# A selective scan: the products with B on GpSimd, those with C on VectorE, decay and states in PSUM

## The chip, the cores and the metric

The kernel runs on one core of a Trainium2 chip. A core has a matrix engine (TensorE, "PE" in the profile, its weight loads "PEld"), VectorE ("DVE"), ScalarE ("ACT"), GpSimd ("POOL") and SyncE ("SP", which issues the DMAs here). Each runs its own list of instructions in order and waits on semaphores for the others. [...] The metric is the device time of one execution, in microseconds. The kernel before takes 18,649.57 us, the median of three runs (18,648.17 to 18,655.98).

## The reference

The input is 2 images of 96 channels and 128 x 128 points. Layer 0 normalizes over the channels and adds a mixing step: four Mamba scans (along rows, along columns, and both in reverse), each with 192 inner channels and 16 states a channel, whose outputs are projected and summed. A feed-forward net of 96, 384 and 96 with quantized numbers follows; layer 1 is a 3 x 3 convolution and another such net. Only the scan matters here:

```python
dt = softplus(dt_raw @ dt_w.T + dt_b)          # per channel and point
dA = exp(dt[:, :, None] * A)                   # A = -exp(A_log), 16 per channel
h  = dA * h + dt[:, :, None] * B[:, None, :] * u[:, :, None]
y  = einsum('bds,bs->bd', h, C)                # sum over the 16 states
y  = y + Dp * xc                               # the skip; xc is u
y  = y * silu(z)
return y @ outp_w.T
```

B and C (16 values a point each) and `dt_raw` are projections of `xc`, which is the Silu of a causal convolution of four taps over the projected input.

## The kernel before

Each image goes through three stages: `normalize`, `mamba` (the scans) and `ffn_and_conv`. The sum over the four directions is kept in `acc` in SBUF.

`mamba` runs the four directions as two pairs: rows with columns, forward, then both in reverse. A pair has 384 channels, three groups (`NG`) of 128 partitions; group 1 holds 64 channels of each direction. A step is 512 points of one pair (`T`), so there are 64 steps an image and 128 in all. A step has 24 units: a unit is one group and two of the 16 states, worked on as tiles of 128 x 2 x 512.

A unit before the change (`inputs_of` and `scans`, lines 277 to 301):

- TensorE broadcasts the two B rows to all partitions by matmuls with 0/1 weights `sel` into the PSUM tile `bc` (L282). B is split in three bf16 parts, `parts`, for accuracy (L229 to L239).
- ScalarE makes the decay `da` = exp(dt x A) in SBUF, one instruction a state (L285).
- VectorE multiplies `bc` by `dtu` = dt x u in place (L290) and runs two scans over the 512 points (L293), which write the states `h` in SBUF.
- ScalarE copies the last point's state to `hst`, for the next step (L297).
- GpSimd multiplies `h` by the C rows `cs` (L299). `cs` comes by DMA: the C rows are written to DRAM (L222) and read back, broadcast to 128 partitions (L274), three units ahead (`AHEAD`).
- TensorE adds the product to the group's sum `y` in PSUM by a matmul with the identity (L301).

After a group's eight units `finish` (L303) adds the skip on VectorE (L308), multiplies by the gate on GpSimd (L309) and, after groups 1 and 2, projects with TensorE and adds into `acc` with VectorE (L318, L320, L326).

The inputs of a step (`prologue`, L185) are made in the step before, piece by piece: after each unit one more piece of a generator is written. It loads two input tiles (L196), runs the convolution as 16 matmuls (L182), Silu (L206), the gates (L211), the projections to C rows (L218) and to B and dt (L228), and per group the softplus (L246 to L260), of which ScalarE makes Abs, Relu, Exp and Ln, VectorE a rounding step `q` (L255), and GpSimd three sums and `dtu` (L258 to L262). ScalarE loads another function table before the Silus and back after them (L206, L213).

What sets the order: every engine but ScalarE gets its instructions from a planner, which starts from the written order and may move an instruction that it holds to be ready ahead of one that waits; ScalarE keeps the written order in `mamba` (L329). Waits follow from which instructions touch which tiles. [...]

Of the kernel before, what the change touches and what calls it, by code (L numbers as in the profile page):

```python
# [1 line left out]

# [17 lines left out]
C = 96  # L20
# [11 lines left out]
AHEAD = 3  # L32
DTO = 96
# [3 lines left out]
def tile_metaformer(ctx: ExitStack, tc: tile.TileContext, a: dict, out: bass.AP):  # L37
# [21 lines left out]
    bdw = const("bdw", (128, 2, NG, DTO + 2 * RK))  # L59
    cw = const("cw", (128, 2, NG, 2 * S))  # L60
    dtw = const("dtw", (2 * RK, 2, NG * 128))
    dtb = const("dtb", (128, 2, NG))
    dskip = const("dskip", (128, 2, NG))
# [4 lines left out]

    amat = cpool.tile([128, 2, NG, S], F32, name="amat")
    sel = cpool.tile([96, S, 2, 128], BF16, name="sel")  # L70
# [3 lines left out]
    with tc.tile_pool(name="prep", bufs=1) as pp, tc.tile_pool(name="prep_ps", bufs=2, space=PSUM) as pps:  # L74
# [4 lines left out]
        onehot = pp.tile([96, 2, S], F32, name="onehot")  # L79
        nc.sync.dma_start(onehot, a["onehot"])  # L80
        for d in range(2):
            nc.vector.tensor_copy(sel[:, :, d, :], onehot[:, d, :, None].broadcast_to((96, S, 128)))
# [75 lines left out]
    def mamba(acc, xnr, xnc):  # L158

        with ExitStack() as st:  # L160
            pool = lambda n, bufs, **kw: st.enter_context(tc.tile_pool(name=n, bufs=bufs, **kw))
            io, one, two, gen = pool("io", 2), pool("one", 1), pool("two", 2), pool("gen", 6)
            ps_bc, ps_y, ps_m = (pool(n, k, space=PSUM) for n, k in (("ps_bc", 2), ("ps_y", 1), ("ps_m", 3)))
# [21 lines left out]
            def prologue(pi, i, d):  # L185

                rev = pi == 1
                lo = L - (i + 1) * T if rev else i * T
                src = []
                for n, dram in (("xa", xnr), ("xb", xnc)):  # L190
                    t = io.tile([C, T + 3], F32, name=n)
                    if i == 0:
                        nc.gpsimd.memset(t[:, T : T + 3] if rev else t[:, 0:3], 0.0)
                        nc.sync.dma_start(t[:, 0:T] if rev else t[:, 3 : T + 3], dram[:, lo : lo + T])
                    else:
                        nc.sync.dma_start(t, dram[:, lo : lo + T + 3] if rev else dram[:, lo - 3 : lo + T])  # L196
                    src.append(t[:, ::-1] if rev else t)
                yield
                d["xc"], d["sz"], d["dt"], d["dtu"] = [], [], [], []
                ps = []  # L200
                for g in range(NG):
                    ps.append(inproj(pi, g, lambda dd, k, lo, hi: inx[:, dd, k, lo:hi], src, (0, 1, 2, 3)))
                    yield
                for g in range(NG):
                    xc = gen.tile([128, T], F32, name="xc")
                    nc.scalar.activation(xc, ps[g], AF.Silu, bias=convb[:, pi, g : g + 1])  # L206
                    d["xc"].append(xc)
                for g in range(NG):
                    z = inproj(pi, g, lambda dd, k, lo, hi: inz[:, dd, lo:hi], src, (3,))
                    sz = gen.tile([128, T], F32, name="sz", bufs=5)  # L210
                    nc.scalar.activation(sz, z, AF.Silu)  # L211
                    d["sz"].append(sz)
                nc.scalar.preload_act_table_set("natural_log_exp_and_others")  # L213
                yield

                ps = misc()
                for g in range(NG):
                    nc.tensor.matmul(ps[0 : 2 * S, :], cw[:, pi, g, :], d["xc"][g], start=g == 0, stop=g == NG - 1)  # L218
                crow = one.tile([2 * S, T], F32, name="crow")
                nc.scalar.copy(crow, ps[0 : 2 * S, :])  # L220
                d["cd"] = rows_d.tile([2 * S, T], F32, name="cd")
                nc.sync.dma_start(d["cd"], crow)  # L222
                yield


                ps = misc()
                for g in range(NG):
                    nc.tensor.matmul(ps[0 : DTO + 2 * RK, :], bdw[:, pi, g, :], d["xc"][g], start=g == 0, stop=g == NG - 1)  # L228
                parts = two.tile([96, T], BF16, name="parts")  # L229
                nc.scalar.copy(parts, ps[0:96, :])  # L230
                rest = one.tile([96, T], F32, name="rest")
                nc.vector.tensor_tensor(rest, ps[0:96, :], parts, ALU.subtract)
                dtr = one.tile([2 * RK, T], F32, name="dtr")
                nc.scalar.copy(dtr, ps[DTO : DTO + 2 * RK, :])
                yield
                mid = one.tile([96, T], BF16, name="mid")
                nc.gpsimd.tensor_copy(mid, rest)
                nc.vector.tensor_copy(parts[32:64, :], mid[32:64, :])
                nc.gpsimd.tensor_tensor(parts[64:96, :], rest[64:96, :], mid[64:96, :], ALU.subtract)  # L239
                d["parts"] = parts  # L240
                yield


                for g in range(NG):
                    ps = misc()
                    nc.tensor.matmul(ps, dtw[:, pi, g * 128 : (g + 1) * 128], dtr, start=True, stop=True)  # L246
                    bias = dtb[:, pi, g : g + 1]
                    e = one.tile([128, T], F32, name="e")
                    nc.scalar.activation(e, ps, AF.Abs, bias=bias)
                    dt = gen.tile([128, T], F32, name="dt", bufs=4)  # L250
                    nc.scalar.activation(dt, ps, AF.Relu, bias=bias)  # L251
                    nc.scalar.activation(e, e, AF.Exp, scale=-1.0)
                    yield
                    q = one.tile([128, T], F32, name="q")
                    nc.vector.tensor_scalar(q, e, 1.0, 1.0, ALU.add, ALU.subtract)  # L255
                    ln = one.tile([128, T], F32, name="ln")
                    nc.scalar.activation(ln, e, AF.Ln, bias=1.0)
                    nc.gpsimd.tensor_tensor(q, e, q, ALU.subtract)  # L258
                    nc.gpsimd.tensor_tensor(ln, ln, q, ALU.add)  # L259
                    nc.gpsimd.tensor_tensor(dt, dt, ln, ALU.add)  # L260
                    dtu = gen.tile([128, T], F32, name="dtu", bufs=4)
                    nc.gpsimd.tensor_tensor(dtu, dt, d["xc"][g], ALU.mult)  # L262
                    d["dt"].append(dt)
                    d["dtu"].append(dtu)
                    yield

            def c_rows(d, g, s):

                cs = gen.tile([128, 2, T], F32, name="cs", bufs=4)
                for half in range(2) if g == 1 else (slice(None),):  # L270
                    rows = slice(half * 64, half * 64 + 64) if g == 1 else half
                    at = s + S * (half if g == 1 else g // 2)
                    n = 64 if g == 1 else 128
                    nc.sync.dma_start(cs[rows], d["cd"][None, at : at + 2, :].broadcast_to((n, 2, T)))  # L274
                return cs

            def inputs_of(pi, d, g, s):

                bp = ps_bc.tile([128, 2, T], F32, name="bc")
                for j in range(2):  # L280
                    w = sel[:, s + j, :, :].rearrange("k d m -> k (d m)")[:, 64 * g : 64 * g + 128]
                    nc.tensor.matmul(bp[:, j, :], w, d["parts"], start=True, stop=True)  # L282
                da = two.tile([128, 2, T], F32, name="da")
                for j in range(2):
                    nc.scalar.activation(da[:, j, :], d["dt"][g], AF.Exp, scale=amat[:, pi, g, s + j : s + j + 1])  # L285
                return bp, da

            def scans(i, d, g, s, y, cs, bp, da):

                nc.vector.tensor_tensor(bp, d["dtu"][g][:, None, :].broadcast_to((128, 2, T)), bp, ALU.mult)  # L290
                h = two.tile([128, 2, T], F32, name="h")
                for j in range(2):
                    nc.vector.tensor_tensor_scan(  # L293
                        h[:, j, :], da[:, j, :], bp[:, j, :],
# [3 lines left out]
                hc = two.tile([128, 2, T], F32, name="hc")  # L298
                nc.gpsimd.tensor_tensor(hc, h, cs, ALU.mult)  # L299
                for j in range(2):  # L300
                    nc.tensor.matmul(y, ident, hc[:, j, :], start=s + j == 0, stop=s + j == S - 1)  # L301

            def finish(pi, i, d, g, y):  # L303

                rev = pi == 1
                lo = L - (i + 1) * T if rev else i * T
                t = one.tile([128, T], F32, name=f"yg{g}")
                nc.vector.scalar_tensor_tensor(t, d["xc"][g], dskip[:, pi, g : g + 1], y, ALU.mult, ALU.add)  # L308
                nc.gpsimd.tensor_tensor(t, t, d["sz"][g], ALU.mult)  # L309
                d["yg"].append(t[:, ::-1] if rev else t)  # L310
                yg = d["yg"]
# [22 lines left out]
            for _ in prologue(*steps[0], state[0]):  # L334
                pass
            cs = {k: c_rows(state[0], *units[k]) for k in range(AHEAD)}
            got = inputs_of(steps[0][0], state[0], *units[0])
            for n, (pi, i) in enumerate(steps):
# [3 lines left out]
                for u, (g, s) in enumerate(units):  # L342
# [7 lines left out]
                    else:  # L350
                        for _ in ahead:
                            pass
# [157 lines left out]
```

## Time and profile before

| | us |
|---|---|
| median of three runs | 18,649.57 |
| the profiled execution | 18,639.52 |
| its span, first to last instruction | 18,637.7 |
| VectorE busy | 12,812.0 |
| TensorE busy (matmuls) | 14,287.1 |
| GpSimd busy | 10,041.0 |
| ScalarE busy | 6,766.3 |

The 40 slices of the page show where the stages are. Two long even stretches are the scans of the two images; the short ones between and at the end, in which GpSimd is nearly idle, are the feed-forward nets with the convolution:

```profile
DVE  4777777777777777753347777777777777777533
POOL 2666666666666666630026666666666666666300
DMA  2333333333333333310023333333333333333100
```

In a line of the groups, the part before the first bar says what instruction it is (line, engine, operation, tile written <- tiles read, shapes, count), then come busy us in total and mean ns of one, then the idle time of that engine just before such instructions and whom it waited for. Busy time counts a stretch once, also where two instructions of an engine overlap.

### The profile page before, as it was taken

Reading aid. Unit: us, or ns where it says so; the run is one execution under the profiler, and the core shown is the slowest. Engines: PE = TensorE matmul, PEld = TensorE weight load, DVE = VectorE, ACT = ScalarE, POOL = GpSimd, SP = SyncE. Lnnn points to the kernel's source line nnn. Section 1 sums busy time; section 2 is a strip of 40 time slices with the busy share of each in tenths; the row PEclk is TensorE's granted clock in tenths of the full one; section 3 lists DMA queues with packets and bytes.
Section 4 is the critical chain, followed back from the end, with each engine's and each line's share of the span. In section 5 each row is a group of like instructions: output and inputs, shape, how many; then the busy total and the mean of one; then the engine's idle time right before and its main releaser. Section 6 shows DMA issues by size and latency. Waiting matters only on the chain. (4 is left out here: it accounts for less than half of the span.)

```text
span 18637.7 us, 119806 instructions
## 1 busy us (share of the span) xinstructions
PE 14287.1 (77%) x33424; PEld 5080.7 (27%) x33424; DVE 12812.0 (69%) x12267; ACT 6766.3 (36%) x13205; POOL 10041.0 (54%) x5412
## 2 busy tenths in 40 slices
PE   6777777777777777777767777777787777777777
PEld 2222222222222222223322222222222222222233
DVE  4777777777777777753347777777777777777533
ACT  2433333343333433422223433333333334334222
POOL 2666666666666666630026666666666666666300
PEclk7888998899988888877778889988888888888777
DMA  2333333333333333310023333333333333333100
GB/s 87 109 105 108 108 107 108 105 108 108 107 106 106 106 106 106 107 55 6 6 85 106 108 106 108 108 107 106 106 107 107 104 107 106 108 106 106 54 6 6
DMA packets 511015, 1732.76 MB, mean 93 GB/s; under 512 B 75612, under 2 KB 76988, under 8 KB 505640
## 3 DMA queue, kind: packets, MB, share of 16 engines
q1 hardware_dynamic: 510344, 1725.11, 29.9%
q8 instruction: 263, 4.31, 0.1%
q14 instruction: 408, 3.34, 0.1%
HBM read 1678.68 MB, written 46.14 MB: 93 GB/s over the span
## 5 line engine op out<-in xcount | busy, mean ns | idle before, releaser
L299 POOL TENSOR_TENSOR hc<-h,cs 128x1024 f32<-128x1024 f32 x3072 | 7245.3, 2362 | 5219.9 <-DVE h L293 3434.5
L301 PE MATMUL y<-hc,ident 128*128 128x512 f32 x12288 | 7260.5, 722 | 2487.3 <-POOL hc L299 2456.2
L293 DVE TENSOR_TENSOR_SCAN h<-da,hst,bc 128x512 f32<-128x512 f32 x5952 | 7218.0, 1262 | 211.0 <-ACT da L285 72.9
L290 DVE TENSOR_TENSOR bc<-dtu,bc 128x1024 f32<-128x1024 f32 x3072 | 3685.8, 1219 | 2206.1 <-PE bc L282 2198.5
L301 PEld LDWEIGHTS y<-hc,ident 128*128 128x128 f32 x12288 | 2534.1, 224 | 6549.6 <-POOL hc L299 4297.4
L285 ACT ACTIVATE da<-dt,amat 128x512 f32<-128x512 f32 x6144 | 4080.7, 712 | 1.5
L297 ACT COPY hst<-h 128x2 f32<-128x2 f32 x3072 | 586.0, 191 | 7922.3 <-DVE h L293 7922.1
L282 PE MATMUL bc<-parts,sel 96*128 96x512 bf16 x6144 | 1970.8, 396 | 571.7 <-DVE h L293 568.4
L416 POOL TENSOR_TENSOR acc<-acc,y 96x512 f32<-96x512 f32 x128 | 147.0, 1148 | 2158.8 <-DVE y L415 2158.8
L282 PEld LDWEIGHTS <-sel 96*128 96x128 bf16 x6144 | 598.6, 102 | 2583.7 <-issue 2521.4
L182 PE MATMUL misc<-xa,inx 96*128 96x512 f32 (+1 forms) x2048 | 1054.8, 611 | 64.0 <-issue 32.2
L182 PE MATMUL misc<-xb,inx 96*64 96x512 f32 (+1 forms) x2048 | 1047.6, 610 | 0.3 <-ACT dt L251 0.3
L308 DVE SCALAR_TENSOR_TENSOR yg<-xc,dskip,y 128x512 f32<-128x512 f32 x384 | 285.3, 743 | 745.8 <-PE y L301 745.8
L309 POOL TENSOR_TENSOR yg<-yg,sz 128x512 f32<-128x512 f32 x384 | 485.5, 1264 | 543.9 <-DVE yg L308 486.8
L431 PE MATMUL pc<-pad,kw 96*96 96x512 f32 x1152 | 663.0, 699 | 48.2 <-DVE pad L129 48.2
L126 PE MATMUL pr<-sd,bcast_w 128*96 128x128 f32 x2048 | 450.1, 390 | 313.5 <-DVE sd L123 309.5
L114 ACT ACTIVATE sq<-xm 96x512 f32<-96x512 f32 x256 | 161.0, 629 | 1202.6 <-DVE xm L112 1161.1
L211 ACT ACTIVATE sz<-misc 128x512 f32<-128x512 f32 x384 | 229.3, 597 | 996.7 <-POOL yg L309 656.3
L260 POOL TENSOR_TENSOR dt<-dt,ln 128x512 f32<-128x512 f32 x384 | 490.9, 1278 | 20.2
L259 POOL TENSOR_TENSOR ln<-ln,q 128x512 f32<-128x512 f32 x384 | 485.5, 1264 | 30.1
L262 POOL TENSOR_TENSOR dtu<-dt,xc 128x512 f32<-128x512 f32 x384 | 486.6, 1267 | 27.8
L258 POOL TENSOR_TENSOR q<-e,q 128x512 f32<-128x512 f32 x384 | 484.7, 1262 | 9.6 <-DVE q L255 9.6
(88 smaller groups left out, 9731.6 us busy)
## 6 DMA issues: line engine op xcount, KB each, us to landing
cs<-cd SPq DMA_DIRECT2D x2048, 512.0 KB, 3.7
cs<-cd SPq DMA_DIRECT2D x2048, 256.0 KB, 3.9
xa<-xnr SPq DMA_DIRECT2D x124, 193.1 KB, 3.4
xb<-xnc SPq DMA_DIRECT2D x124, 193.1 KB, 4.0
acc<-in_x_dram SPq DMA_DIRECT2D x16, 768.0 KB, 16.2
xnr<-xn SPq DMA_DIRECT2D x16, 768.0 KB, 4.3
xnc<-st SPq DMA_DIRECT2D x16, 768.0 KB, 4.6
out_dram<-acc SPq DMA_DIRECT2D x64, 192.0 KB, 2.1
```

The source lines that it names most:

```text
L182: nc.tensor.matmul(ps[rows, :], w(PAIRS[pi][d], k, lo, hi), src[d][:, k : k + T], **se)
L259: nc.gpsimd.tensor_tensor(ln, ln, q, ALU.add)
L260: nc.gpsimd.tensor_tensor(dt, dt, ln, ALU.add)
L262: nc.gpsimd.tensor_tensor(dtu, dt, d["xc"][g], ALU.mult)
L282: nc.tensor.matmul(bp[:, j, :], w, d["parts"], start=True, stop=True)
L285: nc.scalar.activation(da[:, j, :], d["dt"][g], AF.Exp, scale=amat[:, pi, g, s + j : s + j + 1])
L290: nc.vector.tensor_tensor(bp, d["dtu"][g][:, None, :].broadcast_to((128, 2, T)), bp, ALU.mult)
L293: nc.vector.tensor_tensor_scan(h[:, j, :], da[:, j, :], bp[:, j, :], 0.0 if i == 0 else hst[:, g, s + j : s + j + 1], ALU.mult, ALU.add,)
L297: nc.scalar.copy(hst[:, g, s : s + 2], h[:, :, T - 1])
L299: nc.gpsimd.tensor_tensor(hc, h, cs, ALU.mult)
L301: nc.tensor.matmul(y, ident, hc[:, j, :], start=s + j == 0, stop=s + j == S - 1)
L431: nc.tensor.matmul(pc, kw[:, t, :], rows, start=t == 0, stop=t == 8)
```

## The change

- The B and C rows now both come by DMA. One projection (`bcw`) makes dt, B and C together; B and C rows alternate in DRAM (`bcd`), and a unit's load is four rows, B and C of two states, into one SBUF tile `bc` of 128 x 2 x 2 x 512. Five such tiles are in turn, and loads are issued three units ahead (`ROWS_AHEAD`). The broadcast by TensorE, `sel`, `parts`, `rest` and `mid` go.
- GpSimd multiplies B by `dtu`, in place in `bc`, two units ahead (`AHEAD`).
- `da` is a PSUM tile (three of two banks, six of the eight banks). The scans write the states over it, and VectorE multiplies them with C, in place in `bc`.
- Four units of 24 (`BY_POOL`) are treated otherwise: their scans write the states over B in SBUF, and GpSimd makes the product with C one unit later.
- The skip is a matmul of `xc` with a diagonal matrix `dmat`, which starts the sum `y`; the gate is then one product on VectorE (`gated`), after the first unit of the next group. Projection and adding into `acc` come two and three units after a group.
- The pieces of the prologue are tied to fixed units by a table (`at`). Convolution and gate leave PSUM through Identity and copy, and two long Silus over three groups each follow in SBUF. `misc` has one buffer.

The core of the diff (imports, constants and host-side layout left out; of the prologue, what moves to new functions unchanged is left out):

```diff
+ROWS_AHEAD = 3
+AHEAD = 2
+BY_POOL = ((0, 2), (0, 6), (0, 10), (1, 2))
...
-            io, one, two, gen = pool("io", 2), pool("one", 1), pool("two", 2), pool("gen", 6)
-            ps_bc, ps_y, ps_m = (pool(n, k, space=PSUM) for n, k in (("ps_bc", 2), ("ps_y", 1), ("ps_m", 3)))
+            io, one, two, gen = pool("io", 2), pool("one", 1), pool("two", 2), pool("gen", 4)
+            ps_w, ps_y, ps_m = (pool(n, k, space=PSUM) for n, k in (("ps_w", 3), ("ps_y", 1), ("ps_m", 1)))
...
+                def conv(g):
+                    ps = inproj(pi, g, lambda dd, k, lo, hi: inx[:, dd, k, lo:hi], src, (0, 1, 2, 3))
+                    if g == 0:
+                        d["xc"] = two.tile([128, NG, T], F32, name="xc")
+                    nc.scalar.activation(d["xc"][:, g, :], ps, AF.Identity, bias=convb[:, pi, g : g + 1])
+                def gate(g):
...
+                    nc.scalar.copy(d["sz"][:, g, :], ps)
+                def silu():
+                    for t in (d["xc"], d["sz"]):
+                        nc.scalar.activation(t, t, AF.Silu)
+                    nc.scalar.preload_act_table_set("natural_log_exp_and_others")
+                def rows():
...
+                    nc.scalar.copy(d["rows"], ps[0 : BCO + NBC, :])
+                    d["bcd"] = rows_d.tile([NBC, T], F32, name="bcd")
+                    nc.sync.dma_start(d["bcd"], d["rows"][BCO:, :])
...
+                at = [(0, load), (9, silu), (10, rows)]
+                at += [(k, partial(conv, g)) for g, k in enumerate((2, 3, 4))]
+                at += [(k, partial(gate, g)) for g, k in enumerate((5, 6, 8))]
+                for g, k in enumerate((11, 14, 18)):
+                    for m, f in ((0, dt_in), (1, dt_ln), (2, dt_q), (3, dt_log), (3, dt_sum), (4, dt_u)):
+                        at.append((k + m, partial(f, g)))
+                return sorted(at, key=lambda p: p[0])
+            def bc_rows(d, g, s):
+                bc = gen.tile([128, 2, 2, T], F32, name="bc", bufs=5)
...
+                    src = d["bcd"][None, at : at + 4, :].broadcast_to((n, 4, T))
+                    nc.sync.dma_start(bc[rows].rearrange("p s k t -> p (s k) t"), src)
+            def inputs_of(pi, d, g, s, bc):
+                b = bc[:, :, 0, :]
+                nc.gpsimd.tensor_tensor(b, d["dtu"][g][:, None, :].broadcast_to((128, 2, T)), b, ALU.mult)
+                da = ps_w.tile([128, 2, T], F32, name="da")
                 for j in range(2):
                     nc.scalar.activation(da[:, j, :], d["dt"][g], AF.Exp, scale=amat[:, pi, g, s + j : s + j + 1])
+            def scans(i, d, g, s, bc, da):
+                b, c = bc[:, :, 0, :], bc[:, :, 1, :]
+                by_pool = (g, s) in BY_POOL
+                h = b if by_pool else da
                 for j in range(2):
                     nc.vector.tensor_tensor_scan(
-                        h[:, j, :], da[:, j, :], bp[:, j, :],
+                        h[:, j, :], da[:, j, :], b[:, j, :],
                         0.0 if i == 0 else hst[:, g, s + j : s + j + 1], ALU.mult, ALU.add,
                     )
                 nc.scalar.copy(hst[:, g, s : s + 2], h[:, :, T - 1])
-                hc = two.tile([128, 2, T], F32, name="hc")
-                nc.gpsimd.tensor_tensor(hc, h, cs, ALU.mult)
+                if not by_pool:
+                    nc.vector.tensor_tensor(c, h, c, ALU.mult)
+            def sums(s, y, bc):
                 for j in range(2):
-                    nc.tensor.matmul(y, ident, hc[:, j, :], start=s + j == 0, stop=s + j == S - 1)
+                    nc.tensor.matmul(y, ident, bc[:, j, 1, :], start=False, stop=s + j == S - 1)
+            def by_pool(s, y, bc):
+                nc.gpsimd.tensor_tensor(bc[:, :, 1, :], bc[:, :, 0, :], bc[:, :, 1, :], ALU.mult)
+                sums(s, y, bc)
+            def gated(pi, d, g, y):
                 t = one.tile([128, T], F32, name=f"yg{g}")
-                nc.vector.scalar_tensor_tensor(t, d["xc"][g], dskip[:, pi, g : g + 1], y, ALU.mult, ALU.add)
-                nc.gpsimd.tensor_tensor(t, t, d["sz"][g], ALU.mult)
+                nc.vector.tensor_tensor(t, y, d["sz"][:, g, :], ALU.mult)
...
+            for k in range(total + 4):
+                n, u = divmod(k, nu)
+                if u == 0 and n + 1 < len(steps):
+                    for m, f in prologue(*steps[n + 1], state[n + 1]):
+                        later(k + m, f)
+                fetch(k + ROWS_AHEAD)
+                prepare(k + AHEAD)
+                for f in todo.pop(k, ()):
+                    f()
...
+                scans(i, d, g, s, bc[k], da.pop(k))
+                if s == 0:
+                    if k > 0:
+                        pn = (k - 1) // nu
+                        gated(steps[pn][0], state[pn], units[k - 1 - pn * nu][0], y)
+                    y = ps_y.tile([128, T], F32, name="y")
+                    nc.tensor.matmul(y, dmat[:, pi, g, :], d["xc"][:, g, :], start=True, stop=False)
+                if (g, s) in BY_POOL:
+                    later(k + 1, by_pool, s, y, bc.pop(k))
+                else:
+                    sums(s, y, bc.pop(k))
+                if s == S - 2 and g > 0:
+                    later(k + 2, project, pi, d, g)
+                    later(k + 3, collect, pi, i, d, g)
```

Here `fetch` calls `bc_rows`, `prepare` calls `inputs_of`, and `later(k, f)` writes `f` into the list of unit `k`, which is run after that unit's `prepare` and before its scans.

## The prediction

> **What bounds the kernel now.** First the page, for the shares of the engines (busy us, share of the span, count):
>
> ```profile
> span 18637.7 us, 119806 instructions
> PE 14287.1 (77%) x33424; PEld 5080.7 (27%) x33424; DVE 12812.0 (69%) x12267; ACT 6766.3 (36%) x13205; POOL 10041.0 (54%) x5412
> ```
>
> No engine is full. Next a steady stretch of the scan stage, 700 to 7600 us (busy of PE, PEld, DVE, ACT, POOL, granted clock, DMA share, GB/s):
>
> ```profile
> 700.00:7600.00 6900.00, 5394.85 (x11818) 1852.48 (x11816) 5209.46 (x4609) 2724.18 (x5343) 4326.91 (x2304) 0.89 0.35 107
> ```
>
> The same stretch by lines (count | busy, mean ns | idle before):
>
> ```profile
> L293 DVE TENSOR_TENSOR_SCAN h<-da,hst,bc 128x512 f32<-128x512 f32 x2651 | 3215.0, 1262 | 94.7 <-ACT da L285 32.8 <-DVE bc L290 2.4
> L290 DVE TENSOR_TENSOR bc<-dtu,bc 128x1024 f32<-128x1024 f32 x1349 | 1618.8, 1219 | 966.6 <-PE bc L282 965.8
> L308 DVE SCALAR_TENSOR_TENSOR yg<-xc,dskip,y 128x512 f32<-128x512 f32 x169 | 125.5, 743 | 325.4 <-PE y L301 325.4
> L299 POOL TENSOR_TENSOR hc<-h,cs 128x1024 f32<-128x1024 f32 x1349 | 3181.9, 2362 | 2295.7 <-DVE h L293 1501.4 <-DMA cd<-crow 271.4 <-PE y L301 212.2
> L285 ACT ACTIVATE da<-dt,amat 128x512 f32<-128x512 f32 x2696 | 1790.8, 712 | 0.7
> ```
>
> 1349 products are 56.2 steps of 24 units, so a step takes 6900 / 56.2 = 122.8 us, and 128 steps 15,718 of the span. The rest (normalization, FFN and convolution) the change leaves alone. Per step DVE is busy 92.7, POOL 77.0, PE 96.0, ACT 48.5. DVE's idle 30.1 us are mostly a wait for PE's broadcast of B (965.8 / 56.2 = 17.2) and for PE's sum y (5.8): PE works in order, and the next broadcast stands behind a sum that waits for POOL. The loop DVE, POOL, PE, DVE bounds the step, with DVE as its longest member.
>
> One more row matters. L230 and L234 copy parts of one PSUM tile on ACT, and L232 reads it on DVE between them:
>
> ```profile
> L234 ACT COPY dtr<-misc x128: 579/579/581, 305.7 to 17289.6; 12x512 f32<-12x512 f32 x128
> its engine sat idle before it (us, times) until:
>   DVE rest L232: 284.4, 128
> ```
>
> dtr needs nothing that rest writes; it only reads the same PSUM tile, and it waited 128 times of 128, 2.2 us each. Two engines' reads of one PSUM tile are put in program order here.
>
> **The change, per step.** Durations are means of these rows.
>
> DVE. Out: 24 B products (28.8), three L308 (2.2), L232 (0.66), L238 (0.28); 92.7 - 31.9 = 60.8 stay. In: 20 products with C. Their form (PSUM in, SBUF out, 1024 elements) is not in the trace; the nearest is L290 at 1.219, PSUM to PSUM: 24.4. Three gated products like L320 (0.683): 2.05. Sum 87.2. The scans move their output to PSUM; the rows for a scan are 1203 and 1262 ns, both with one PSUM operand, and L290 writes PSUM at full rate, so I change nothing; 60 ns either way on 48 would be 2.9 us.
>
> POOL. Out: L309 (3.8), mid and its subtraction (1.9). The 24 products with C become 24 with B, same size, 2.362. In: four more with C, 9.4. 77.0 - 5.7 + 9.4 = 80.7, below DVE.
>
> PE. Out: 48 broadcasts (866.4 / 56.2 = 15.4) and one of two row projections (2.8). In: three skip matmuls (six instructions at 0.59, 3.5). 96.0 becomes 81. PE no longer stands between POOL and DVE, so the 17.2 goes; y is read one unit after its last sum, so the 5.8 goes.
>
> ACT. Out: six Silus from PSUM (685 and 597), parts, crow and dtr (574, 569, 579): 5.6. In: three Identity (0.685), three copies (0.57), the rows (0.57), two Silus of 1536 elements. From L77 (96 elements, 282) and L252 (512, 627) one costs 282 + 1440 x 0.83 = 1477 ns. 48.5 becomes 50.2. Exponentials into PSUM have no row; I keep 712.
>
> DMA and SP. Still 32 row loads a step on SP, each twice as long; the row write also doubles, and later loads stand behind it on SP as before. The issues (count, size, median us to landing):
>
> ```profile
> cs<-cd SPq DMA_DIRECT2D x2048, 512.0 KB, 3.7
> cs<-cd SPq DMA_DIRECT2D x2048, 256.0 KB, 3.9
> cd<-crow SPq DMA_DIRECT2D x128, 64.0 KB, 1.6
> ```
>
> And the densest stretch of transfers, the loads of x near the start (columns as in the steady stretch):
>
> ```profile
> 20.00:30.00 10.00, 6.20 (x26) 3.35 (x26) 2.79 (x7) 2.28 (x3) 0.00 (x0) 1.00 1.02 251
> ```
>
> A step moves 24 x 1.05 = 25.2 MB. At the densest stretch, the loads of x at full DMA share, 251 GB/s make 100 us of it. At the steady stretch 107 GB/s took 0.35 of the engines, 306 GB/s at full share: 82 us. The loads are of the second kind (the same rows to all partitions), so I take 82: hidden below DVE, with little room. [...]
>
> The new wait. `da` is now PSUM, the states overwrite it, and both hst's copy (ACT) and the C product (DVE) read it; the copy is first in the program. By L234's row the 20 products wait for the copy. ACT keeps its written order, and ahead of the copy stand two exponentials (1.42) and whatever the prologue puts in that unit. Price: the copy's 0.19 (L297) and two hand-offs of some 0.05 (a scan's end to the copy's start), 0.3 x 20 = 6.0. ACT work ahead: Identity 2.1, copies 1.7, Silus with two table loads (2 x 1.48 + 2 x 1.283) 5.5, rows 0.6, Abs, Relu and Exp (684, 678, 627) 6.0, Ln 1.9: 17.8. That work itself waits for PE, as there is one `misc` buffer instead of three: L182's 921.7 us of busy PE are 16.4 a step, 13.1 of it the convolutions (16 of its 20 matmuls, counting pairs of 64 columns that run together as one: 12 of 15) and 3.3 the gates; rows 2.8, dt 3.5: 22.7. In all 46.5. Cover: while ACT does the exponentials and this work, DVE has its own two scans (2.45 - 1.42 = 1.03 in 14 such units, 14.4), and in three of those units, given to POOL, no product waits at once (about 2). In written order 30 us stay. A planner orders DVE, though, and it does move scans forward: in the timeline (start, us, merged count) four scans, of two units, run in a row:
>
> ```profile
> 3065.57 2.35 DVE L290 TENSOR_TENSOR bc<-dtu,bc 128x1024 f32<-128x1024 f32 x2
> 3067.84 4.79 DVE L293 TENSOR_TENSOR_SCAN h<-da,hst,bc 128x512 f32<-128x512 f32 x4
> ```
>
> The next unit's scans (2.45, its dA made two units ahead) can fill most gaps. So the ends are 0 and 30; before, the planned order still left DVE idle 30.1 of 122.8. I take half, 15. [...]
>
> Of POOL's units: the buffer of row loads (five, held until the sum) is held longer in four units: POOL's B product and own product (4.7), sum (1.99 in the timeline), load (3.7 + 8 packets x 0.159 = 5.0, an estimate), B product again (2.4): 14.1 us against about 13.5 of DVE work in the four units between. It costs 1 to 2 us a step; L255, the one DVE line that reads and writes SBUF alone, is stretched when POOL works (min/median/max ns; its mean is 831), and POOL is busier now:
>
> ```profile
> L255 DVE TENSOR_SCALAR q<-e x168: 396/402/2566, 740.7 to 7508.4; 128x512 f32<-128x512 f32 x168
> L299 POOL TENSOR_TENSOR hc<-h,cs x1349: 2331/2352/2550, 701.0 to 7598.0; 128x1024 f32<-128x1024 f32 x193
> ```
>
> For both I count 3 in the best case, and put them inside the 15 otherwise.
>
> Sum: 87.2 + 15 = 102 us a step, 20.8 less. The profiled execution took 18,639.5 (its span and 1.8), 10 below the median of the three timed runs: 18,650 - 128 x 20.8 = 15,990.
>
> **The rivals.**
> 1. The planner hides the hand-off: 87.2 + 3 = 90, 14,450. For: ACT has 50 of 90 us and dA is ready two units ahead. Against: before, its order left a quarter idle.
> 2. DVE runs as written: 117, 17,910. For: L234 waits every time, and ACT's order is fixed. Against: the reordering in the timeline.
> 3. The same hand-off with no cover at all: 87.2 + 46.5 = 133.7, 20,050, slower. It decides from 35.6 of the 46.5 uncovered (122.8 - 87.2), that is, if DVE finds less than 11 us of other work a step while ACT waits for PE. Against: its own two scans alone cover 14.
> 4. Row loads bound: 100 + 2 for the other transfers, 102, 15,990 like the forecast, but with DMA share near 1.
> 5. POOL and DVE block each other at SBUF: slower once a POOL product takes (122.8 - 14.6) / 28 = 3.9 us (14.6 is POOL's other work). Against: L299 spans 2331 to 2550 while scans with one SBUF operand run, and all new DVE products have one.
>
> **How the numbers follow.** Forecast (92 to 110 a step, 14,710 to 17,010) 0.50; rival 1 0.20; rival 2 (110 to 122.4) 0.16; rival 4 0.04; rivals 3 and 5 0.08; within 0.2% (37 us, what a measurement here can tell) 0.02. Faster 0.90, same 0.02, slower 0.08. Range: from a little under rival 1 (89, 14,350) to rival 2 (17,900), which leaves some 0.07 below and 0.13 above.
>
> **What would show it.** Right: DVE busy near 87 a step and POOL near 81, POOL products still 2.36, no idle for a B broadcast, and DVE's largest wait the C product's for hst on ACT, around the units with prologue work. Wrong: that wait below 3 us a step (rival 1) or ACT waiting for PE in nearly every unit with DVE idle 30 (rivals 2, 3); DMA share over 0.9 (rival 4); POOL products over 3 us (rival 5); scans over 1.3 us.

## The result, and the profile after

The changed kernel took 20,322 us (20,292 to 20,329, 4 runs) against 18,653 (18,648 to 18,659, 4 runs) for the kernel before: 1.089 times as long, 95% interval 1.087 to 1.091. The prediction was 15,990 and faster.

The page of the kernel after: span, busy time of the engines, and the DMA queue's line (packets, MB, share of 16 engines).

```profile
span 20290.5 us, 109103 instructions
PE 13705.2 (68%) x27280; PEld 4793.7 (24%) x27280; DVE 12281.8 (61%) x11503; ACT 7199.8 (35%) x13205; POOL 10428.4 (51%) x5284
q1 hardware_dynamic: 514184, 3343.96, 55.0%
```

Every engine is busy for a smaller share of the span than before. The steady stretch, 700 to 8300 us (columns as in the prediction):

```profile
700.00:8300.00 7600.00, 5126.77 (x9072) 1724.56 (x9072) 4956.92 (x4256) 2900.23 (x5320) 4481.91 (x2243) 0.81 0.63 190
```

and its lines:

```profile
L289 POOL TENSOR_TENSOR bc<-dtu,bc 128x1024 f32<-128x1024 f32 x1345 | 3138.3, 2346 | 913.7 <-DMA bc<-bcd 802.1 <-ACT hst L304 79.4 <-DVE da L300 20.8
L300 DVE TENSOR_TENSOR_SCAN da<-da,hst,bc 128x512 f32<-128x512 f32 x2200 | 2829.3, 1288 | 1919.2 <-POOL bc L289 1553.2 <-issue 314.8 <-DMA bc<-bcd 5.7
L306 DVE TENSOR_TENSOR bc<-da,bc 128x1024 f32<-128x1024 f32 x1120 | 1362.2, 1216 | 271.3 <-ACT hst L304 270.3 <-PE y L310 0.9
L313 POOL TENSOR_TENSOR bc<-bc 128x1024 f32<-128x1024 f32 x224 | 526.4, 2350 | 779.3 <-DVE bc L300 776.6 <-DMA bc<-bcd 2.6
L254 POOL TENSOR_TENSOR q<-e,q 128x512 f32<-128x512 f32 x168 | 212.2, 1263 | 864.4 <-DVE q L249 864.4
```

1345 products are 56.04 steps, so a step takes 135.6 us, 12.8 more than before (x 128 = 1,640 of the 1,669 us). DVE is busy 88.5 of them: its work shrank by 4 us a step and its idle time grew from 30 to 47. The waits in the same stretch (engine and line <- what it waited for: us, times, longest):

```profile
DVE da L300 <- POOL bc L289: 1584.1, 503, 6.0
POOL q L254 <- DVE q L249: 864.4, 168, 7.8
POOL bc L289 <- DMA bc<-bcd: 802.1, 290, 9.6
POOL bc L313 <- DVE bc L300: 776.6, 223, 6.1
DVE bc L306 <- ACT hst L304: 270.3, 610, 1.6
```

PE's broadcast is gone from the list. In its place DVE's scans wait 28 us a step for GpSimd's product with B, and GpSimd waits 29 us a step for DVE (at q and at its own products) and 14 for loads. The loads (count, KB, median us from issue to landing):

```profile
bc<-bcd SPq DMA_DIRECT2D x2048, 1024.0 KB, 4.7
bc<-bcd SPq DMA_DIRECT2D x2048, 512.0 KB, 10.9
bcd<-rows SPq DMA_DIRECT2D x128, 128.0 KB, 8.7
```

Group 1 is loaded by two DMAs of 64 partitions each, half as large as the others and landing more than twice as late; the row write behind them on SP is late too.

### The profile page after: what moved, and what is told of

Same layout as the page of the kernel before. It is cut to its first block, busy times and chain, and to the rows that moved or that the text cites. A ratio compares the mean times of both kernels' runs of the same rounds, so it can differ in the third digit from the quotient of the medians.

```text
span 20290.5 us, 109103 instructions
## 1 busy us (share of the span) xinstructions
PE 13705.2 (68%) x27280; PEld 4793.7 (24%) x27280; DVE 12281.8 (61%) x11503; ACT 7199.8 (35%) x13205; POOL 10428.4 (51%) x5284
## 4 chain that ended last, share of the span: by engine, by line
DVE 26%; PE 21%; POOL 20%; issue 13%; DMA 11%; ACT 9%; SPq 0%; POOLq 0%; DVEq 0%; ACTq 0%
POOL bc L289 13%; DVE da L300 12%; DMA bc<-bcd 10%; PE y L310 8%; DVE bc L306 7%; PE misc L185 4%; DVE bc L300 3%; ACT da L292 3%; PE pc L466 2%; POOL ln L257 2%; PE pr L129 2%; PE pm L113 2%; POOL dt L260 2%; DVE sd L126 1%; POOL dtu L264 1%
## 5 line engine op out<-in xcount | busy, mean ns | idle before, releaser
L310 PE MATMUL y<-bc,ident 128*128 128x512 f32 x12288 | 7859.4, 773 | 4064.9 <-DVE bc L306 4048.8
L300 DVE TENSOR_TENSOR_SCAN da<-da,hst,bc 128x512 f32<-128x512 f32 x4960 | 6378.8, 1288 | 4280.3 <-POOL bc L289 3476.3
L289 POOL TENSOR_TENSOR bc<-dtu,bc 128x1024 f32<-128x1024 f32 x3072 | 7168.6, 2347 | 2092.1 <-DMA bc<-bcd 1811.3
L310 PEld LDWEIGHTS y<-bc,ident 128*128 128x128 f32 x12288 | 2682.7, 237 | 9009.7 <-DVE bc L306 6334.9
L306 DVE TENSOR_TENSOR bc<-da,bc 128x1024 f32<-128x1024 f32 x2560 | 3113.8, 1216 | 623.6 <-ACT hst L304 622.2
L313 POOL TENSOR_TENSOR bc<-bc 128x1024 f32<-128x1024 f32 x512 | 1203.0, 2350 | 1786.0 <-DVE bc L300 1771.8
L300 DVE TENSOR_TENSOR_SCAN bc<-da,hst,bc 128x512 f32<-128x512 f32 x992 | 1224.5, 1265 | 79.7 <-POOL bc L289 79.7
L386 PE MATMUL y<-xc,dmat 128*128 128x512 f32 x768 | 498.2, 734 | 760.3 <-DVE yg L318 760.3
L325 PE MATMUL misc<-yg,gmat 128*96 128x512 f32 x1024 | 633.9, 705 | 211.0 <-ACT dt L243 209.4
L226 PE MATMUL misc<-xc,bcw 128*96 128x512 f32 x768 | 492.8, 794 | 227.0 <-ACT xc L219 227.0
## 6 DMA issues: line engine op xcount, KB each, us to landing
bc<-bcd SPq DMA_DIRECT2D x2048, 512.0 KB, 10.9
```

The lines of the kernel that those rows point to most:

```text
L289: nc.gpsimd.tensor_tensor(b, d["dtu"][g][:, None, :].broadcast_to((128, 2, T)), b, ALU.mult)
L300: nc.vector.tensor_tensor_scan(h[:, j, :], da[:, j, :], b[:, j, :], 0.0 if i == 0 else hst[:, g, s + j : s + j + 1], ALU.mult, ALU.add,)
L306: nc.vector.tensor_tensor(c, h, c, ALU.mult)
L310: nc.tensor.matmul(y, ident, bc[:, j, 1, :], start=False, stop=s + j == S - 1)
L313: nc.gpsimd.tensor_tensor(bc[:, :, 1, :], bc[:, :, 0, :], bc[:, :, 1, :], ALU.mult)
L325: nc.tensor.matmul(d["po"], gmat[:, pi, 2 * g - 2 + k, :], d["yg"][g - 1 + k], start=k == 0, stop=k == 1)
```

## The experiments

Three suspects came out of these views, named in the expectations as theories D, P and H: group 1's slow loads (D; the edit that repairs them is called L below), the place of GpSimd's instructions in its queue (P; the edit that tests it is called P too), and the product's wait for the copy to hst, which the prediction had priced (H; the edit is C). Times are medians; runs without an interval are single ones, beside which the kernel before took 18,618 to 18,651 us. An edit can also make the planner order the engines anew; where the trace shows that, the text says so.

**GpSimd in written order (P).** The planner had moved GpSimd's own products and its part of the prologue forward: in its queue q stands behind B product 11, 14 and 20 of a step, where the program writes it behind 15, 18 and 22, and then waits for DVE.

```
- manual_schedule(engines={Activation})
+ manual_schedule(engines={Activation, Pool})
```

> One edit: GpSimd, like ScalarE, keeps the written order. Three theories of the 13 us a step that the change adds. P (GpSimd's order): its later work, the four products with C and the softplus sums, was moved ahead of B products that VectorE needs at once, and waits there for VectorE or ScalarE; VectorE idles 34.7 us a step for B. H (hand-off): VectorE's C products wait for ScalarE's copy of the last state. D (row loads): group 1's loads land late (10.9 us). P expects most of the 34.7 to go: 103 to 115 us a step for 135.6, 16,200 to 17,700 us. H and D expect no change: 20,000 to 20,600.

20,185 us, 1.082 [1.081, 1.084] of before: only 137 less than the kernel after, so theory P missed by far. GpSimd's 29 us a step of waits for DVE at q and at its own products were gone, but its wait for loads rose from 14 to 44 (2174.3 us over 49.8 steps).

**The copy to hst after the product (C).**

```
-                nc.scalar.copy(hst[:, g, s : s + 2], h[:, :, T - 1])
                 if not by_pool:
                     nc.vector.tensor_tensor(c, h, c, ALU.mult)
+                nc.scalar.copy(hst[:, g, s : s + 2], h[:, :, T - 1])
```

> One edit: the copy of the last state is written after VectorE's C product, so that the product no longer waits for ScalarE. H expects 10 us a step or more to go: 19,000 or less. P expects the 4.9 us of VectorE's waits for the copy to become waits for B: 19,900 to 20,400. D the same as P.

20,396, no gain: 74 more than the kernel after. But the planner's order of GpSimd, VectorE and TensorE changed with the edit, so this isn't the copy's place alone.

**No products with C on GpSimd**, all 24 on VectorE.

```
-BY_POOL = ((0, 2), (0, 6), (0, 10), (1, 2))
+BY_POOL = ()
```

> One edit: no unit's C product goes to GpSimd, VectorE makes all 24. P expects VectorE's idle time after the four GpSimd units (18.4 us a step) to go and four products (4.9) to come: 13 us less, 18,650, and between 18,200 and 19,400. H expects four more products with hand-off: 5 to 6 us more, about 21,000. D expects within 2 us a step of no change, 20,050 to 20,600.

20,135, so 187 less: P's 13 us a step did not come, and these four units are not the cause by themselves.

**One load for group 1.**

```
-                for half in range(2) if g == 1 else (slice(None),):
-                    ...
+                at = 2 * (s + S * (g // 2))
+                src = d["bcd"][None, at : at + 4, :].broadcast_to((128, 4, T))
+                nc.sync.dma_start(bc.rearrange("p s k t -> p (s k) t"), src)
```

> One edit, and the output changes: group 1's rows are loaded by one DMA to 128 partitions instead of two to 64, all with the rows of the first direction, so half of group 1 gets the other direction's B and C. D expects GpSimd's waits for loads (14.3 us a step) to go, and the step to fall by 8 to 14: 18,500 to 19,300. P expects these waits to be mostly covered or passed on: 19,700 to 20,350. H: no change.

18,190, 2,132 less, more than theory D expected. The stretch 700 to 7400 of this run, and two of its waits:

```profile
700.00:7400.00 6700.00, 4924.60 (x9147) 1670.43 (x9146) 5035.71 (x4276) 2865.41 (x5348) 4522.99 (x2252) 0.86 0.58 216
```

```profile
POOL bc L286 <- DMA bc<-bcd: 874.8, 546, 6.7
DVE da L297 <- POOL bc L286: 843.5, 527, 4.9
```

The step is 119 us and DVE's wait for the B product halved (15 a step). But the planner's order had changed with the edit (in GpSimd's queue, q now stands behind B product 14, 17 and 21), so the load is not alone in this number. The next two runs fix every engine to the written order, first with the loads of the kernel after, then with one load.

```
- manual_schedule(engines={Activation})
+ manual_schedule(engines={Activation, Pool, DVE, PE, SP})
```

> All five engines keep the written order; nothing else changes. After the first four runs theory D is sharpened: group 1's loads go to 64 partitions at a time, their 8 KB packets take 625 ns instead of 309, so a unit's two loads hold the DMA engines 5.0 us where the unit has 3.7 of VectorE work, and the ring of five buffers falls behind. D expects the order to matter little while the loads stay: 19,600 to 21,500. P (the planner's order, of VectorE and TensorE too and not of GpSimd alone) expects 16,500 to 18,300.

> All engines in written order, and group 1's rows by one DMA to 128 partitions (half of group 1 gets the other direction's B and C, so the output changes). Against the run with written order alone the order of instructions is now the same but for that load, which it was not in the first run with one load. D expects 10 to 20 us a step less than that run. P expects under 3 us less.

20,327 and 18,980: in one and the same order the load is worth 1,347 us, 10.5 a step. With the loads of the kernel after, the planner's order as a whole is no better or worse than the written one (20,322); with one load, the new order that the planner made is 789 us faster (18,190). In the written order the product's wait for the copy is in full view (stretch 700 to 7400; first the two loads, 49.5 steps, then the one, 53.5):

```profile
POOL bc L289 <- DMA bc<-bcd: 2362.0, 663, 9.3
DVE bc L306 <- ACT hst L304: 1884.6, 988, 12.8
```

```profile
POOL bc L286 <- DMA bc<-bcd: 1955.3, 738, 8.2
DVE bc L303 <- ACT hst L301: 1527.8, 1067, 7.3
```

38 and 29 us a step.

**What makes the two loads slow?** A second queue for the upper half, whose load ScalarE issues, and quarters of 32 partitions:

```
-                    nc.sync.dma_start(bc[rows]...
+                    (nc.scalar if g == 1 and half else nc.sync).dma_start(bc[rows]...
```

```
-                for half in range(2) if g == 1 else (slice(None),):
+                for lo in (0, 64, 32, 96) if g == 1 else (0,):
```

> [...] D expects packets of 309 to 450 ns and most of the gain of the one-load run: 18,100 to 19,300. P expects no gain: 20,000 to 20,600. If ScalarE is held by the wait ahead of its issue, the kernel gets slower than the change under either.

> The changed kernel, but group 1's unit is loaded by four DMAs of 32 partitions, lower and upper halves in turn (0, 64, 32, 96), all from SP. D expects part of the overlap that 4 KB packets showed before (235 where 159 is undisturbed): packets of 350 to 550 ns, 18,300 to 19,800. If two in turn on one queue do not overlap: 20,100 to 20,600. P: 20,100 to 20,600.

19,465 and 22,093, both outside what any theory expected. With two queues the time fell by 857 us, but a packet of 8 KB still takes some 640 ns in the trace, as with one queue (some 625), against 309 in a load of 128 partitions; both halves land in 7.2 us. The planner's order changed here too (q again behind B product 14, 17 and 21), so what the second queue itself is worth isn't shown. Quarters (some 570 ns, landing in 7.2 us too) are little faster, and SP waits for them besides (695 us in all). Then the same two loads, each to every second partition:

```
-                    rows = slice(half * 64, half * 64 + 64) if g == 1 else half
+                    rows = slice(half, 128, 2) if g == 1 else half
```

> Group 1's two row loads write every second partition (0, 2, 4, ... and 1, 3, 5, ...) in place of the lower and the upper 64; count, size, order and queue of the loads stay, and so does all other work. The channels are not moved with them, so in group 1 half of the channels get the B and C of the other direction. Theory D (a load to 64 neighbouring partitions runs at half rate because of where it writes): packets of 8 KB fall from about 625 to about 310 ns, group 1's loads land in under 6 us, and the time comes near that with one load for group 1: 18,000 to 18,500 us. Rival (splitting is what costs: a load of 64 rows has half the packets per DMA engine, wherever it writes): packets stay near 600 ns, time 20,200 to 20,400.

The packets fell to 309 ns and the loads landed in 4.5 us instead of 10.9; same packets and bytes, less time:

```profile
q1 hardware_dynamic: 514184, 3343.96, 44.7%
bc<-bcd SPq DMA_DIRECT2D x2048, 1024.0 KB, 4.7
bc<-bcd SPq DMA_DIRECT2D x2048, 512.0 KB, 4.5
```

So the rate here went with which partitions a load writes, as theory D said: 309 ns a packet where it writes every second partition, some 625 where it writes 64 neighbours. Why neighbours are slower no run here shows. Yet the time, 19,987, is far above the 18,000 to 18,500 of theory D and a little under its rival's range: with every engine in exactly the order of the kernel after, repairing the loads alone brings 335 us. The same with all engines in written order:

> All engines in written order, and group 1's two loads write every second partition (half of group 1's channels get the other direction's B and C). All-written order alone gave 20,327 us, with one load for group 1 18,980. Theory D (the rate of the packets is what the one load changed): 18,850 to 19,200. Rival (the number of loads is): over 19,900.

19,136: there the rate is worth 1,191 of the 1,347 us. The load matters much in one order and little in the other, which pointed at a second limit.

**The full computation with interleaved channels**: even partitions of group 1 hold one direction, odd ones the other; weights padded with zeros do it, and the loads are those of the run above.

```
-                        ((0, slice(0, 64), 128, 192), (1, slice(64, 128), 0, 64)),
...
-                        nc.tensor.matmul(ps[rows, :], w(PAIRS[pi][d], k, lo, hi), src[d][:, k : k + T], **se)
+                halves = (0, 1) if g == 1 else (g // 2,)
...
+                        nc.tensor.matmul(ps, w(g, d, k), src[d][:, k : k + T], **se)
```

> The full computation with group 1's channels interleaved: even partitions hold the pair's first direction, odd ones the second, by weights padded with zeros, so that group 1's two loads write every second partition. Added: group 1's convolution and gate run as ten products of 128 columns where pairs of 64 columns ran together, about 5 x 0.8 = 4 us of PE a step. Theory D: 18,000 to 18,900 us (the interleaved loads' time and up to 4 us a step), that is 0.965 to 1.013 of the kernel before. Rival (splitting costs, not the place): 20,200 to 20,900.

20,461, 1.097 [1.095, 1.099]: slower, with GpSimd in the planner's order, the same as in the kernel after. The time is in the rival's range, though the packets of the interleaved run had already ruled out the rival's reason.

**A sixth row buffer**, with one load for group 1:

```
-                bc = gen.tile([128, 2, 2, T], F32, name="bc", bufs=5)
+                bc = gen.tile([128, 2, 2, T], F32, name="bc", bufs=6)
```

> One load for group 1 (half of its channels get the other direction's B and C) and six buffers of row loads in place of five. Theory R (with one load the ring of five is what still keeps the step at 119 us: GpSimd waits 15.5 us a step for loads): step 105 to 112, 16,400 to 17,400 us, GpSimd's wait for loads under 6 us a step. Rival M (PE's one misc buffer, ACT's written order and the lower PE clock keep it): over 17,900 us, with ACT's wait for the convolutions still near 18 us a step.

17,511 against 18,190, between both theories: a step of 113.8 instead of 118.9, and GpSimd's wait for loads hardly changed. The planner moved GpSimd's instructions here as well (q behind B product 14, 18 and 22), so the 5 us a step aren't the buffer's alone.

**The three suspects together.** L is the interleaved loads alone (half of group 1's channels get the other direction's B and C, the amount of work stays), P and C are the edits above.

> Both suspects removed at once: group 1's two loads write every second partition (half of group 1's channels get the other direction's B and C), and GpSimd runs in written order. Alone, the first gave 19,987 us and the second 20,185. Theory T (two limits, each enough to hold the step near 133 us: the slow loads, and GpSimd's planned order): 18,000 to 18,900 us. Rival A (neither matters, the gains just add): 20,322 - 335 - 137 = 19,850, give or take 100.

> As the run before, and the copy to hst is written after the product with C instead of ahead of it (half of group 1's channels get the other direction's B and C). Theory H (once loads and GpSimd's order are out of the way, the product's wait for ACT's copy is what binds, as in the all-written order with one load, where it left VectorE idle about 30 us a step): 5 to 12 us a step less than the run before, 16,500 to 18,000 us. Rival (the planner hides it anyway, as with the kernel after, where the same edit gave +74): within 150 us of the run before.

> GpSimd in written order and the late copy to hst, with the row loads as in the kernel after (64 neighbouring partitions). Theory T (the half-rate loads alone hold the step): 19,700 to 20,300 us, near the 20,185 of GpSimd's order alone. Rival (the late copy is what brought 17,753, the loads hardly matter): under 19,200.

> Group 1's two loads write every second partition (half of its channels get the other direction's B and C) and the copy to hst comes after the product, with GpSimd in the planner's order. Theory T (GpSimd's planned order alone holds the step): 19,600 to 20,200 us, near the 19,987 of the interleaved loads alone. Rival (the order hardly matters once loads are fast and the copy late): 17,600 to 18,300. The late copy can also change the planner's order; then neither number holds, and GpSimd's order against its B products tells it.

| edits | us | | edits | us |
|---|---|---|---|---|
| none | 20,322 | | P | 20,185 |
| L | 19,987 | | P, L | 18,819 |
| C | 20,396 | | P, C | 18,970 |
| L, C | 20,392 | | P, L, C | 17,753 |

In the planner's order neither L nor C nor both bring more than 335 us. With GpSimd in written order L brings 1,366 and C 1,215, and together they bring 2,432, almost the sum. Read the other way, P is worth 137 us alone and 2,638 once L and C are in. So theory T was right that GpSimd's order holds the step (though 20,392 is above its 19,600 to 20,200), and its claim that the slow loads alone hold it fell (it expected 19,700 or more of P with C): they are one term of a sum. Of the edits, L is the clean one. It leaves the order of every engine as it was in all four pairs, and is worth 335, 5, 1,366 and 1,217 us. P and C make the planner order VectorE and TensorE anew, so their numbers hold that too.

The trace says what is added up. Matching the k-th load, B product, pair of scans and C product of the stretch 700 to 6800 gives the life of a row buffer, from its load's issue to the next load's issue into the same buffer (mean us; units whose landing the trace has):

| edits | load lands | waits, B product | waits, 2 scans | to end of C product | sum, next issue | round | x 24 / buffers |
|---|---|---|---|---|---|---|---|
| none | 7.2 | 5.9 + 2.4 | 1.9 + 2.7 | 4.0 | 4.2 | 28.3 | 136 |
| L, C | 4.8 | 11.1 + 2.4 | 2.7 + 2.6 | 1.5 | 3.4 | 28.4 | 136 |
| P | 7.2 | 1.1 + 2.4 | 0.9 + 2.9 | 8.6 | 5.1 | 28.1 | 135 |
| P, L | 5.5 | 1.1 + 2.4 | 1.4 + 2.9 | 8.2 | 4.4 | 25.9 | 124 |
| P, L, C | 5.8 | 1.7 + 2.4 | 2.8 + 2.7 | 3.4 | 5.3 | 24.1 | 116 |

Five buffers in turn serve 24 units a step, so 24/5 of a round is a step by construction, whatever holds it: the last column tests the matching and doesn't prove that the ring of buffers binds. Where the ring binds, each us of waiting in a unit costs 4.8 us a step. Where something else does, a us saved comes back as another wait: in the planner's order what L and C save (2.4 and 2.5 us) comes back as the wait of a landed load for GpSimd (5.9 to 11.1). The waits of L with C, stretch 700 to 7400 (49.2 steps), show why:

```profile
DVE da L300 <- POOL bc L289: 1760.1, 443, 6.2
POOL bc L313 <- DVE bc L300: 1362.5, 196, 11.0
POOL q L254 <- DVE q L249: 877.0, 147, 7.7
POOL bc L289 <- DMA bc<-bcd: 40.0, 48, 1.3
```

Loads are hardly waited for (0.8 us a step); GpSimd stands 46 us a step before its own products and q, behind DVE, and DVE 36 us behind GpSimd's B products, which are queued behind those. So the eight runs fit two limits at nearly the same height, GpSimd's order at some 135 us (L with C, 136) and the round of the buffers with slow loads and the early copy (P alone, 135), which is why each edit alone showed next to nothing.

**The repair.** Interleaved channels, GpSimd in written order, late copy, in the full computation, with five and with six row buffers (the sixth made room for by three dtu buffers in place of four):

```
-                    dtu = gen.tile([128, T], F32, name="dtu")
+                    dtu = gen.tile([128, T], F32, name="dtu", bufs=3)
...
-                bc = gen.tile([128, 2, 2, T], F32, name="bc", bufs=5)
+                bc = gen.tile([128, 2, 2, T], F32, name="bc", bufs=6)
```

> The full computation with interleaved channels, GpSimd in written order and the late copy to hst, with the five buffers of row loads of the kernel after (and four of dtu). Theory R (the ring of five still costs): 17,300 to 17,900 us, 1,000 to 1,600 over the version with six, as the run with these three edits alone gave 17,753. Rival (something else in the rewritten weights brought it): 16,200 to 16,500.

> The full computation: group 1's channels interleaved (weights padded with zeros), GpSimd in written order, the copy to hst after the product, six buffers of row loads in place of five, three of dtu in place of four. If theories T and H hold: the time of the run with the late copy, and up to 4 us a step for PE's extra products, less up to 5 for the sixth buffer: 16,000 to 18,200 us, faster than before. If both rivals hold: 19,500 to 20,000.

17,725 with five and 16,240 (16,232 to 16,257) with six: 0.872 [0.870, 0.873] of the kernel before, faster than both. Theory R held: the sixth buffer is worth 1,484 us, 11.6 a step. GpSimd's order is the same in both; VectorE's and TensorE's were planned anew. The six-buffer kernel, 700 to 6800 us (58.9 steps of 103.5), and three of its waits:

```profile
700.00:6800.00 6100.00, 4819.34 (x9542) 1803.42 (x9542) 5259.02 (x4475) 3068.60 (x5591) 4726.65 (x2359) 0.92 0.67 249
```

```profile
POOL bc L281 <- DMA bc<-bcd: 1064.9, 418, 8.5
ACT xc L201 <- PE misc L177: 850.7, 177, 9.2
DVE da L292 <- POOL bc L281: 135.9, 107, 5.4
```

DVE is busy 89.3 of 103.5 us and waits 2 us a step for the B product. GpSimd still waits 18 us a step for loads, with little effect on DVE. A seventh buffer wasn't tried; what keeps the last 14 us is open, ACT's wait for PE's convolutions (14 a step) being one candidate.

## Why the prediction was wrong

**The work was priced right.** DVE 87.2 a step, measured 88.5; GpSimd 80.7, measured 80.0; ACT 50.2, measured 51.8. The B product on GpSimd took 2.35 us (2.36), the C product on DVE 1.216 (1.219), a merged Silu 1.47 to 1.48 (1.477). PE was busy 91.5 instead of 81, with the sum's matmul at 774 ns in place of 720, at a granted clock of 0.81 instead of 0.89. The 17.2 us for PE's broadcast and 5.8 for y did go. Scans in PSUM took 1288 instead of 1262, inside the 60 ns allowed for.

**Two steps failed. The first is the ring's: "It costs 1 to 2 us a step".** It set 14.1 us of holding time, made of bare durations and for four units alone, against 13.5 us of DVE work. Two things were left out. The ring holds every unit, so its round had to be compared with 5/24 of the step: 18.2 us for 87.2. And in that round each wait counts. Bare, it is 14.2 us from rows of the kernel after (load 4.7, B product 2.35, scans 2.6, hand-off and product 1.4, the sum's four matmuls of 774 ns 3.1); only 4 us of waiting a unit are free. Measured were 28.3, the step seen from a buffer, with 14 us of waiting in it. That the ring costs is shown by the sixth buffer, 11.6 us a step in the repaired kernel. L and C, which take waits out of the round, are worth 2,432 us together with GpSimd in written order, 19 a step. No run gave the kernel after a sixth buffer and nothing else.

**The loads: "so I take 82: hidden below DVE, with little room".** The total was about right, 0.63 x 135.6 = 85, but by accident: the uniform rate hid that group 1's halves ran at half of it, some 625 ns a packet against 309 (with interleaved partitions the same bytes took 0.51 x 133 = 68). And the share was the wrong question. What counted was the time to landing, 10.9 us where "5.0, an estimate" stood for every unit, inside the ring. The row was there: before, 256 KB to 64 partitions took 3.9 us against 3.7 for 512 KB. For the same reason rival 4, which wanted a DMA share near 1, named a resource that did matter, with the wrong sign to look for. Nor were the two rates at full share that the price was made of, 251 and 306 GB/s, a limit of these loads: the six-buffer repair moved 249 GB/s at a DMA share of 0.67, an estimated 372 at full share (249 / 0.67).

**The hand-off to ACT: 46.5, 30 in written order, 15 taken.** The size was right where it could be seen: 29 and 30 us a step in written order with fast loads, 38 with slow ones, where 988 of 990 products waited, as L234's row had it. Planned, it measured 4.8, below the 15 and near rival 1, which had called it hidden. It wasn't saved: in written order DVE waits 38 us for the copy and 0.4 for GpSimd's B product (19.3 us in 49.5 steps), planned 4.8 and 28, and the time is the same. The prediction had treated waits as additions to DVE's work, so that hiding one was gain; here it only moved. Moving the copy brought nothing in the kernel after, and 8.3 us a step once GpSimd's order and the loads were repaired.

**The second step that failed is GpSimd's: "80.7, below DVE".** It counted GpSimd's work and put its waits at nothing, without a reason. In the kernel after GpSimd waits 29 us a step for DVE, at q and at its own products, and behind these in its queue stand the B products of the following units, for which DVE waits 28. Once the loads and the copy are repaired, its order is worth 2,638 us, 21 a step.

**The rivals.** None gave this. Rival 3 has nearly the time, 20,050, by a wait that hardly occurred. Rivals 1 and 2 fell with the step at 135.6; rival 5 with GpSimd's product at 2.35, and q on DVE was even less stretched, 431 ns in place of 831. (With GpSimd in written order q is stretched: 1,033 ns with P alone, 1,619 in the five-buffer repair, both from 700 to 6800 us, against 424 in the kernel after. At three a step this is some 2 to 3.5 us.) That the repaired kernel (103.5 us a step, 16,240) lands near the forecast (102, 15,990) does not make it right: its terms are others.

## What to carry to other kernels

For every ring of buffers, add up one buffer's whole round, from the issue of its load to the next, with the waits of the queues in it, and compare buffers / units x step with it: an engine's busy time is a bound only if the ring allows it. When one edit at a time shows nothing, two limits of the same height may stand side by side; undo them in pairs before you drop a cause. Where a planner orders the instructions, compare the orders in the two traces before you credit an edit with the time: here the single edits with the largest effects had changed the order too. And look at loads that write part of the partitions by themselves: here those to 64 neighbours moved half the bytes and landed in 3.9 us against 3.7 before, in 10.9 against 4.7 after.

## What was not expected of the hardware

- Two loads of 64 partitions each had packets of 309 ns, like a load of 128, where each wrote every second partition, and of twice that where each wrote neighbours (some 625, and 640 in two queues); those of 32 neighbours were little better (some 570).
- ACT's exponentials into PSUM took 692 ns instead of 712 into SBUF, and its copy of two columns out of PSUM 156 instead of 191. DVE's scan in place in PSUM took 1288 instead of 1262.
- The granted TensorE clock was 0.81 in the kernel after, where PE was busy 67% of the stretch, and 0.92 in the repaired kernel, where it was busy 79%; the sum's matmul went from 774 to 660 ns. The busy share alone doesn't tell it: the five-buffer repair had 0.90 at 74%, the kernel before 0.89 at 78%. What sets the clock no run here shows.
